# Half-bank pieces in a transformer block: the first exponential of a step in two operations, products and additions by 256 columns

## The chip, the cores and the metric

The kernel runs on one core of one Trainium2 chip. The core has five engines with queues of their own: TensorE (PE, matrix products into PSUM; its weight loads are listed apart as PEld), VectorE (DVE), ScalarE (ACT, exponentials and copies), GpSimd (POOL) and SyncE (SP, which issues the transfers). PSUM has eight banks of 512 fp32 columns over 128 partitions; SBUF is the working memory. The metric is the device time of one execution in microseconds (us). TensorE's weights for one product (`lhsT`) are loaded by an instruction of their own, and it can be addressed as four groups of 32 rows or four groups of 32 columns that work side by side.

## The reference

The input `x` has 8 batches of 1024 tokens and 256 features. All is fp32.

```python
mod = (silu(c) @ wmod).reshape(8, 6, 1, -1)
sa, ca, ga, sb, cb, gb = ...          # shifts, scales, gates; |gates| at least 0.25
h = layernorm(x) * (1 + ca) + sa
x = x + ga * attention(h)             # 16 heads of 16, causal softmax, output projection, bias
h = layernorm(x) * (1 + cb) + sb
x = x + gb * ffn(h)
# ffn, with the token before: h_prev
xr = mu_r * h + (1 - mu_r) * h_prev
xk = mu_k * h + (1 - mu_k) * h_prev
out = sigmoid(xr @ W_r.T) * (square(relu(xk @ W_k.T)) @ W_v.T)
```

## The kernel before

**Units and steps.** A unit is one batch and four of its heads; there are 32. The 1024 tokens are two chunks of 512 (`CW`), each of four blocks of 128 tokens. The attention of a unit goes in nine steps (`STEPS`, `ORDER`): five for blocks on the causal diagonal (a to e; b and d pair a piece of 128 queries with one of 384, c has two of 256) and four for whole blocks of the second chunk's queries against the first chunk's keys (0 to 3).

**What one step does.** `step` (L1122) interleaves two streams of score products on TensorE. The maxima of a later step (`maxima`, tiles `k,q` in the profile, nine steps ahead) put queries by keys into banks, and VectorE finds each row's largest. The weights of the present step (`weights`, tiles `q,k` and `m,ones`) put keys by queries into four banks, subtract the row's maximum by a third product, and `exponentials` (L685) turns each bank of 512 columns into weights `w` in SBUF by one ScalarE operation. The four heads make two halves of two heads, so there are four exponentials in a step, and POOL masks those on the diagonal. Score products use 32 rows of the array (forms `32*128`), so two heads of one stream and two of the other run side by side; the loop at L1149 to L1152 takes the next product from the half that has `took` fewer columns so far.

**What stands between the score products.** After a step's scores come the products in its slot (`fill`) and the attention `attend` (L710) of steps that are done: weights times values, four heads in four groups of 32 columns (form `128*32`). The slots hold the projections of the next batch (`qk`, `v`), the output projection of the batch before (`project`), and its feed-forward part (`receptance`, `key`, `multiplied`, `valued`), placed by tables of step numbers (`POST`, `PREP` and others). `by_strips` (L434) cuts such a product in four strips of 32 columns of the array. A product of fp32 shows as twice as many matmuls in the profile as in the program; the scores, fp32r, as one each.

**Order.** The lines of the code set the order on TensorE throughout. While `strict[0]` is set, which is nearly all of the kernel, they set it on every engine (`InOrder`; all operations therefore show one line, L160). Transfers go through `later` and `transfers` at the start of a step.

**Banks.** All PSUM is one tile, `banks` (L98). `bank` gives the bank that by the kernel's own account is free earliest, and `banks_of_step` plans those of a step's scores, with the first exponential's bank free first. So the first product after a step's scores, be it a projection, a transpose or an attention, commonly takes over the bank that the step's first exponential reads. The semaphore waits are made by the framework from what each instruction reads and writes.

**The edges.** `late[0]` is set from the step where no maxima are left (L1128): the last nine steps. A tail with operations of its own ends the kernel.

Of the kernel before, what the change touches and what calls it, by code (L numbers as in the profile page):

```python
# [10 lines left out]
AF = mybir.ActivationFunctionType  # L11
ALU = mybir.AluOpType
# [3 lines left out]
P = 128  # L16
# [37 lines left out]
FIRST, LAST = ("a", "f", "g"), ("e", "h", "i")  # L54
LAG = 9
BANKS = 8
PIECES = {0: NT, 1: 2 * NT}


# [15 lines left out]
def adaln_block(  # L75
# [235 lines left out]
    def v_tile(b, i):  # L311
        return v_of[(b * NC + i // NT) % (2 * NC)][:, i % NT]
# [141 lines left out]
                )  # L454


    def prep(b, c):
        S = A[b, c]

        def stats(*ts):  # L460
            statistics(S["xa"], S, f"a{b}_{c}", ts)

        def norm(half):
            normalise(S["xa"], S, f"a{b}_{c}", half)
            if half == 0:
                return
            nxt = b * NC + c + 1
            if 1 < nxt < B * NC:
                later(lambda: load_xa(nxt // NC, nxt % NC))

        def turn():
            S["hT"] = sb.tile([P, DC, CW], F32, tag="hT", bufs=2, name=f"hT{b}_{c}")
            for d in range(DC):
                name = f"pta{b}_{c}_{d}"
                transposed(S["h"], S["hT"][:, d, :], b, d, SHIFT_A, SCALE_A, name)

        def qk(n, half):

            pq = bank(f"pq{b}_{c}_{n}_{half}")
            at = n * D + half * P  # L480
            for d in range(DC):
                by_strips(
                    pq, wqk_sb[:, d, at : at + P], S["hT"][:, d, :], d == 0, d == DC - 1
                )
            w, hi = (
                sb.tile([P, CW], F32, tag="qk", bufs=4, name=f"qk{b}_{c}_{n}_{half}{h}")
                for h in range(2)
            )
            if n == 0:
                act.mul(w, pq, SCALE)  # L490
            else:
                act.copy(w, pq)
            hi, lo = hi.bitcast(F32R), w.bitcast(F32R)
            pool.tensor_copy(hi, w)
            pool.tensor_sub(lo, w, hi.bitcast(F32))

            def away():
                to = (q_in, k_in)[n][b % 2][half]
                for h, of in enumerate((hi, lo)):
                    sync.dma_start(to[:, h, c * CW : (c + 1) * CW], of.bitcast(F32))  # L500

            later(away)

        def v(t0):
            pv = bank(f"pv{b}_{c}_{t0}")
            rows(pv, S["hT"], wv_sb, (t0, t0 + 1))
            to = v_of[(b * NC + c) % (2 * NC)]
            act.copy(
                to[:, t0 : t0 + 2, : H * (HD + 1)].rearrange(
                    "p t (h e) -> p t h e", e=HD + 1  # L510
                )[:, :, :, :HD],
                pv.rearrange("p (t h e) -> p t h e", t=2, e=HD),
            )

        return dict(
            stats0=lambda: stats(0, 1),
            stats1=lambda: stats(2, 3),
            stat0=lambda: stats(0),
            stat1=lambda: stats(1),
            stat2=lambda: stats(2),  # L520
            stat3=lambda: stats(3),
            norm0=lambda: norm(0),
            norm1=lambda: norm(1),
            turn=turn,
            q0=lambda: qk(0, 0),
            k0=lambda: qk(1, 0),
            q1=lambda: qk(0, 1),
            k1=lambda: qk(1, 1),
            v0=lambda: v(0),
            v2=lambda: v(2),  # L530
        )
# [127 lines left out]
    def weights(u, k, half, pws):  # L659

        diagonal = STEPS[k][0][2]
        V = U[u]
        qs, kk = qs_of[u % KEPT], k_of[u % KEPT]
        js = (2 * half, 2 * half + 1)
        pw = pws[half]
        parts, total = parts_of(k)
        rounds = []
        for c, kt, lo, cols in parts:
            for h in range(3):

                def products(c=c, kt=kt, lo=lo, cols=cols, h=h):
                    for n2, j in enumerate(js):
                        at = j * ST
                        if h < 2:
                            rs = slice(at, at + ST)
                            left = kk[rs, kt * P : (kt + 1) * P]
                            right = qs[h][rs, c * CW + lo : (c + 1) * CW]
                        else:
                            left = ones[at : at + 2, :]
                            right = V["m", c][at : at + 2, lo:]  # L680
                        pe.matmul(pw[n2][:, cols], left, right, start=h == 0, stop=h == 2)

                rounds.append((CW - lo, products))

        def exponentials():  # L685
            w = sb.tile([P, 2, CW], F32, tag="w", bufs=8, name=f"w{u}_{k}_{half}")
            for n2 in range(2):
                act.activation(w[:, n2, :total], pw[n2][:, :total], AF.Exp)
            if diagonal:

                blocks = len(parts)
                apart = parts[-1][3].start or CW
                on = w.rearrange("p h (m q) -> p h m q", q=apart)[:, :, :blocks, :P]
                pool.affine_select(
                    out=on,
                    in_=on,
                    pattern=[[0, 2], [0, blocks], [1, P]],
                    compare_op=ALU.is_ge,
                    fill=0.0,
                    base=0,  # L700
                    channel_multiplier=-1,
                )
            V["w", k, half] = w

        return rounds, exponentials, 0
# [4 lines left out]
    def attend(u, k, then):  # L710

        c, steps, _ = groups_of(u)[k]
        V = U[u]
        b, g = divmod(u, NG)
        po = bank(f"po{u}_{k}")

        parts = sorted(
            ((at, *part[1:]) for at in steps for part in parts_of(at)[0] if part[0] == c),
            key=lambda part: part[2],
        )  # L720
        ws = {(at, half): V["w", at, half] for at in steps for half in range(2)}
        for m, (at, kt, lo, cols) in enumerate(parts):
            for j in range(HG):
                pe.matmul(
                    po[j * ST : (j + 1) * ST, lo:],
                    v_tile(b, kt)[:, (g * HG + j) * (HD + 1) :][:, :ST],
                    ws[at, j // 2][:, j % 2, cols],
                    start=m == 0,
                    stop=m == len(parts) - 1,
                )  # L730
        then()
        if ("o", c) not in V:
            V["o", c] = sb.tile([P, CW], F32, tag="o", bufs=3, name=f"o{u}_{c}")
            act.copy(V["o", c], po)
        elif strict[0]:
            more = sb.tile([P, CW], F32, tag="more", bufs=2, name=f"more{u}_{k}")
            act.copy(more, po)
            pool.tensor_add(V["o", c], V["o", c], more)
        else:
            dve.tensor_add(V["o", c], V["o", c], po)  # L740
# [88 lines left out]
    def post(b, c):  # L829
# [11 lines left out]
        def flat(t0):  # L841
            return S["x"][:, t0 : t0 + 2, :].rearrange("p t e -> p (t e)")

        def project(t0):
            py = bank_apart(f"py{b}_{c}_{t0}")
            rows(py, S["oT"], G[b]["wo"], (t0, t0 + 1))
            dve.tensor_add(flat(t0), flat(t0), py)

        def stats(*ts):
            statistics(S["x"], S, f"b{b}_{c}", ts)  # L850
# [55 lines left out]

        def key(e):
            pk = bank_apart(f"pk{b}_{c}_{e}")
            for d in range(DC):
                by_strips(  # L910
                    pk, wk_sb[:, d, e * P : (e + 1) * P], S["step"][:, d, :], d == 0, d == DC - 1
                )
            if e == 0:
                S["ka"] = sb.tile([P, DC, CW], F32, tag="mix", bufs=2, name=f"ka{b}_{c}")
            ka = S["ka"][:, e, :]
            act.activation(ka, pk, AF.Relu)
            pool.tensor_mul(ka, ka, ka)
# [7 lines left out]
        def valued(t0):  # L925
            r, pv = S["r", t0], S["pv", t0]

            dve.scalar_tensor_tensor(r, r, 1.0, pv, ALU.add, ALU.mult)
            pool.tensor_add(flat(t0), flat(t0), r)
            if t0:  # L930
                later(lambda: sync.dma_start(tokens(out, b, c), S["x"]))
# [190 lines left out]
    def step(T, T1, S, now, fill):  # L1122
# [26 lines left out]
        while any(lists):  # L1149
            s = min((s for s in range(2) if lists[s]), key=lambda s: (took[s], lists[s][0][3], s))  # L1150
            cols, products, after, _ = lists[s].pop(0)
            took[s] += cols  # L1152
            products()
            if after:
                after()
# [290 lines left out]
```

## Time and profile before

| | |
|---|---|
| time, median of 3 runs | 1377.53 us (1376.43 to 1382.0) |
| the profiled execution | 1386.23 us, its span 1384.5 us |
| granted TensorE clock, mean | 0.961 |
| DVE busy | 1056.9 us (76%) |
| ACT busy | 861.5 us (62%) |
| exponential of 512 columns | 0.60 us |
| DMA engines' mean busy share in a slice | 0 to 0.5 |

A row of the profile names engine, operation, tiles (`out<-in`, buffer numbers left out), shape and count, then the busy time and the mean duration. In the timeline a row begins with start and length in us, rows of the same kind that follow each other are merged (`x4`), and the brackets tell how long the engine was idle before and what released it. In the list of waits a row is: who waited for whom, us in total, times, longest. Matmuls are pipelined and the profile models their ends; their starts are recorded. A few per cent of the matmul records can be missing.

### The profile page before, as it was taken

The page shows a single profiled execution, that of the slowest core. Times are in us where ns is not written, and L with a number is a line of the kernel's source. Part 1 is how long each engine was busy: PE and PEld are TensorE (multiplying, and loading weights), DVE is VectorE, ACT ScalarE, POOL GpSimd, SP SyncE. Part 2 cuts the span into 40 slices and gives each one's busy share as a digit, 9 for nine tenths or more (in the row PEclk, how much of TensorE's full clock was granted, in tenths as well). Part 3 has the DMA queues.
Part 4 walks back from the last instruction along what each step waited for, and adds up shares of the span by engine and source line. Part 5 has one row for each costly group of instructions (what it writes and reads, how often), then busy time and mean ns, then how long its engine had stood idle before and what let it go on. Part 6 is the DMA issues. An engine that isn't in the chain of part 4 may idle for free.

```text
span 1384.5 us, 41749 instructions
## 1 busy us (share of the span) xinstructions
PE 1284.9 (93%) x16570; PEld 692.5 (50%) x16570; DVE 1056.9 (76%) x2910; ACT 861.5 (62%) x1679; POOL 710.7 (51%) x1088
## 2 busy tenths in 40 slices
PE   7898999999999899998999899998999989999988
PEld 4354555544455445554455454554455544544546
DVE  5776777788777877778777888778878788778745
ACT  2475677757567566765666666675666656656562
POOL 1334646546355556455565555564644556555352
PEclk8998999999999999999999999999999999999999
DMA  5114434422344323332434213443223323220111
GB/s 164 68 55 140 163 117 134 147 91 71 106 156 132 96 89 111 132 113 94 129 125 145 92 64 125 149 139 98 85 93 132 133 95 114 95 93 31 51 36 35
DMA packets 86515, 146.70 MB, mean 106 GB/s; under 512 B 12200, under 2 KB 42792, under 8 KB 86320
## 3 DMA queue, kind: packets, MB, share of 16 engines
q1 hardware_dynamic: 86112, 143.84, 31.4%
q8 instruction: 130, 2.13, 0.6%
q14 instruction: 65, 0.53, 0.1%
q10 hardware_dynamic: 208, 0.20, 0.0%
HBM read 86.35 MB, written 56.08 MB: 103 GB/s over the span
## 4 chain that ended last, share of the span: by engine, by line
PE 66%; DVE 9%; POOL 8%; ACT 7%; issue 5%; DMA 0%; POOLq 0%; DVEq 0%; ACTq 0%; SPq 0%
PE banks L160 66%; DVE mix L160 4%; ACT w L160 3%; DVE max L160 2%; POOL qk L160 2%; ACT w_e L160 1%; DVE banks L160 1%; POOL o L160 1%; POOL xb L160 1%; ACT w_d L160 1%; POOL oT L160 1%; POOL w_c L160 1%; POOL w_b L160 1%; POOL mrow L160 1%; POOL w_a L160 0%
## 5 line engine op out<-in xcount | busy, mean ns | idle before, releaser
L160 DVE CUSTOM_DVE_ANT_0 banks<-banks,mask 128x256 f32<-128x256 f32 (+3 forms) x1024 | 467.0, 525 | 121.9 <-PE banks L160 119.4
L160 PE MATMUL banks<-k,q 32*128 32x512 f32 (+3 forms) x3072 | 427.3, 371 | 5.8 <-DVE k L160 3.7
L160 PE MATMUL banks<-q,k 32*128 32x512 f32 (+3 forms) x3072 | 398.1, 369 | 5.4 <-ACT hT L160 1.2
L160 DVE TENSOR_REDUCE max<-banks 128x2 f32<-128x1024 f32 x256 | 302.5, 1221 | 91.7 <-PE banks L160 91.5
L160 PEld LDWEIGHTS banks<-q,k 32*128 32x128 f32 x3072 | 236.5, 185 | 149.0 <-ACT w L160 43.5
L160 ACT ACTIVATE w<-banks 128x512 f32<-128x512 f32 x512 | 264.2, 603 | 61.7 <-PE banks L160 58.4
L160 PE MATMUL banks<-m,ones 2*128 2x512 f32 (+3 forms) x1536 | 262.0, 351 | 8.7 <-DMA m<-mrow 8.7
L160 PEld LDWEIGHTS banks<-k,q 32*128 32x128 f32 x3072 | 252.0, 185 | 29.9 <-DVE max L160 5.9
L160 PEld LDWEIGHTS banks<-m,ones 2*128 2x128 f32 x1536 | 144.7, 185 | 16.1 <-DMA m<-mrow 7.1
L160 DVE DVE_READ_ACCUMULATOR2_ANT max<- 128x1 f32 x1024 | 143.2, 140 | 0.0
L160 PE MATMUL banks<-hT,wqk_sb 128*32 128x512 f32 x960 | 117.6, 610 | 10.6 <-ACT w_b L160 5.0
L160 PE MATMUL banks<-w,v 128*32 128x512 f32 x1024 | 123.2, 599 | 0.4 <-ACT w_a L160 0.2
L160 POOL TENSOR_TENSOR o<-o,more 128x512 f32<-128x512 f32 x62 | 79.2, 1277 | 69.0 <-ACT more L160 69.0
L160 PE MATMUL banks<-wr_sb,mix 128*32 128x256 f32 (+1 forms) x936 | 82.6, 502 | 27.9 <-DVE mix L160 27.7
L160 ACT ACTIVATE w_a<-banks 128x512 f32<-128x512 f32 x128 | 66.1, 602 | 36.3 <-PE banks L160 34.1
L160 POOL TENSOR_TENSOR qk<-qk,qk 128x512 fp32r<-128x512 f32 x60 | 81.0, 1350 | 5.0
L160 ACT ACTIVATE w_c<-banks 128x512 f32<-128x512 f32 x120 | 62.0, 602 | 24.7 <-PE banks L160 24.7
L160 DVE SCALAR_TENSOR_TENSOR mix<-step,mus,h2T 128x512 f32<-128x512 f32 x30 | 75.0, 2532 | 0.0
L160 POOL TENSOR_TENSOR xb<-xb,r 128x512 f32<-128x512 f32 x30 | 39.3, 1311 | 66.4 <-DVE r L160 55.6
L160 ACT ACTIVATE w_e<-banks 128x512 f32<-128x512 f32 x128 | 66.1, 604 | 10.0 <-PE banks L160 9.5
L160 ACT ACTIVATE w_d<-banks 128x512 f32<-128x512 f32 x120 | 62.0, 603 | 16.6 <-PE banks L160 14.6
L160 ACT ACTIVATE r<-banks 128x512 f32<-128x512 f32 x32 | 19.2, 600 | 84.8 <-PE banks L160 81.6
(166 smaller groups left out, 1993.6 us busy)
## 6 DMA issues: line engine op xcount, KB each, us to landing
q<-qin SPq DMA_DIRECT2D x60, 512.0 KB
qin<-qk SPq DMA_DIRECT2D x60, 256.0 KB
kin<-qk SPq DMA_DIRECT2D x60, 256.0 KB
k<-kin SPq DMA_DIRECT2D x30, 512.0 KB
od<-o SPq DMA_DIRECT2D x60, 256.0 KB
xa<-in_x SPq DMA_DIRECT2D x16, 512.0 KB
xb<-in_x SPq DMA_DIRECT2D x16, 512.0 KB
oT<-od SPq DMA_DIRECT2D x60, 128.0 KB
```

Of the source, the lines that this page charges most:

```text
L160: made = f(*args, **kwargs)
```

## The change

Five edits, all of order or of operation size; nothing is computed otherwise.

- The first exponential of each step (first half, first head) is done by two operations, columns 0 to 255 and the rest, while maxima are left (`not late[0]`).
- `columns` does the products of queries, keys and of the feed-forward keys (`qk`, `key`) for 256 columns first and then for the other 256. Before, one matmul had 512 columns.
- `attend` does all products that reach into the first 256 queries, then those of the last 256.
- VectorE adds the output projection to the rows of `x` (`project`) and forms (r + 1) times the values (`valued`) by two operations of 256 columns, while `strict[0]` is set.
- In `step`, a score product counts as at least 256 columns (`SHORT`) when the two halves are interleaved.

```diff
+SHORT = 256
+    def columns(to, lhs, rhs):
+        for of in (slice(0, CW // 2), slice(CW // 2, CW)):
+            for d in range(DC):
+                by_strips(to[:, of], lhs[:, d, :], rhs[:, d, of], d == 0, d == DC - 1)
...
         def qk(n, half):
-            for d in range(DC):
-                by_strips(
-                    pq, wqk_sb[:, d, at : at + P], S["hT"][:, d, :], d == 0, d == DC - 1
-                )
+            columns(pq, wqk_sb[:, :, at : at + P], S["hT"])
...
         def exponentials():
             for n2 in range(2):
-                act.activation(w[:, n2, :total], pw[n2][:, :total], AF.Exp)
+                parted = half == 0 and n2 == 0 and not late[0]
+                for of in (
+                    (slice(0, CW // 2), slice(CW // 2, total)) if parted else (slice(0, total),)
+                ):
+                    act.activation(w[:, n2, of], pw[n2][:, of], AF.Exp)
...
     def attend(u, k, then):
-        for m, (at, kt, lo, cols) in enumerate(parts):
-            for j in range(HG):
-                pe.matmul(
-                    po[j * ST : (j + 1) * ST, lo:],
-                    v_tile(b, kt)[:, (g * HG + j) * (HD + 1) :][:, :ST],
-                    ws[at, j // 2][:, j % 2, cols],
-                    start=m == 0,
-                    stop=m == len(parts) - 1,
-                )
+        for first in range(0, CW, CW // 2):
+            here = [part for part in parts if part[2] < first + CW // 2]
+            for m, (at, kt, lo, cols) in enumerate(here):
+                of = slice(max(lo, first), first + CW // 2)
+                cols = slice(cols.start + of.start - lo, cols.start + of.stop - lo)
+                for j in range(HG):
+                    pe.matmul(
+                        po[j * ST : (j + 1) * ST, of],
+                        v_tile(b, kt)[:, (g * HG + j) * (HD + 1) :][:, :ST],
+                        ws[at, j // 2][:, j % 2, cols],
+                        start=m == 0,
+                        stop=m == len(here) - 1,
+                    )
...
         def project(t0):
-            dve.tensor_add(flat(t0), flat(t0), py)
+            for of in halves():
+                dve.tensor_add(flat(t0)[:, of], flat(t0)[:, of], py[:, of])
+
+        def halves():
+            return (slice(0, D), slice(D, CW)) if strict[0] else (slice(0, CW),)
...
         def key(e):
-            for d in range(DC):
-                by_strips(
-                    pk, wk_sb[:, d, e * P : (e + 1) * P], S["step"][:, d, :], d == 0, d == DC - 1
-                )
+            columns(pk, wk_sb[:, :, e * P : (e + 1) * P], S["step"])
...
         def valued(t0):
-            dve.scalar_tensor_tensor(r, r, 1.0, pv, ALU.add, ALU.mult)
+            for of in halves():
+                dve.scalar_tensor_tensor(r[:, of], r[:, of], 1.0, pv[:, of], ALU.add, ALU.mult)
...
     def step(T, T1, S, now, fill):
-            took[s] += cols
+            took[s] += max(cols, SHORT)
```

## The prediction

> **What bounds the kernel now.** I read the page's busy shares first, then the waits, then the timeline of two typical steps, then the groups by shape.
>
> ```profile
> span 1384.5 us, 41749 instructions
> PE 1284.9 (93%) x16570; PEld 692.5 (50%) x16570; DVE 1056.9 (76%) x2910; ACT 861.5 (62%) x1679; POOL 710.7 (51%) x1088
> PE 66%; DVE 9%; POOL 8%; ACT 7%; issue 5%; DMA 0%; POOLq 0%; DVEq 0%; ACTq 0%; SPq 0%
> ```
>
> TensorE (PE) looks full, and PE holds 66% of the chain. But the ends of matmuls are modelled, so 93% hides short waits. The waits show which:
>
> ```profile
> PEld banks L160 <- ACT w L160: 77.9, 152, 0.9
> ...
> PEld banks L160 <- ACT w_b L160: 36.0, 58, 0.8
> ...
> PEld banks L160 <- ACT w_c L160: 24.5, 29, 2.2
> ...
> PEld banks L160 <- ACT w_a L160: 17.6, 38, 0.8
> ...
> PEld banks L160 <- ACT w_e L160: 14.6, 36, 0.7
> ```
>
> TensorE's next weights wait for an exponential (tiles w, w_a to w_e) 313 times, each time under a microsecond. One such place in the timeline (start, length, engine):
>
> ```profile
> 501.58 2.07 ACT L160 ACTIVATE w_b<-banks 128x512 f32<-128x512 f32 x4 [0.39 <-PE banks L160]
> 501.62 0.34 PE L160 MATMUL banks<-m,ones 2*128 2x384 f32 x2
> 502.23 1.92 PE L160 MATMUL banks<-hT,wqk_sb 128*32 128x512 f32 x16 [0.25 <-ACT w_b L160]
> 504.09 0.39 PE L160 MATMUL banks<-q,k 32*128 32x256 f32 x2
> ```
>
> A step's scores end at 501.62 + 0.34. The first of its four exponentials runs from 501.58 to 502.18 (0.60 us, below). The next product, a projection, starts at 502.23: 0.05 us after that exponential, whose PSUM bank it takes over. Then TensorE runs without a break into the next step at 504.09.
>
> I laid the timeline's PE and ACT rows of the whole span side by side. TensorE has 285 stretches of score products. After 229 of them the next product starts 0.05 us (159 times) or 0.145 us (70 times, mostly products that wait for two engines) after the end of the step's first exponential. No other wait is as regular. So the first exponential's end is on the path some 229 times, and what it gains or loses there moves the whole kernel.
>
> **The change part by part.**
>
> *First exponential in two.* 281 steps get one operation more (the built program has 1758 ACTIVATEs for 1477). Whether the path gains or loses hangs on what the next product waits for. In the built program every such product still has one wait for ScalarE, ahead of its first matmul, and its later matmuls, those of columns 256 to 511 too, have none for ScalarE. Resolving the semaphore counts, 268 of the 274 products that wait for an exponential after a step's scores wait for the second piece; those of before wait for the one operation. The first piece also waits, as before, for the bank's last matmul. So nothing starts earlier, and the product waits for two pieces in a row. Their price, from pairs and singles of the two shapes in the timeline:
>
> ```profile
> 501.58 0.60 ACT L160 ACTIVATE w_b<-banks 128x512 f32<-128x512 f32 x1 [0.39 <-PE banks L160]
> 501.58 1.09 ACT L160 ACTIVATE w_b<-banks 128x512 f32<-128x512 f32 x2 [0.39 <-PE banks L160]
> 1271.74 0.49 ACT L160 ACTIVATE w_f<-banks 128x384 f32<-128x384 f32 x1 [0.18 <-PE banks L160]
> 1271.74 0.87 ACT L160 ACTIVATE w_f<-banks 128x384 f32<-128x384 f32 x2 [0.18 <-PE banks L160]
> ```
>
> Two of 512 columns take 1.09 us, two of 384 take 0.87: 0.215 us per 128 columns and pair. Two of 256 then take 0.87 - 0.215 = 0.66 us. One of 512 takes 0.60. The second piece ends 0.06 us later than the whole did. Bounds: the pieces overlap fully, +0; they don't overlap, 2 x (0.49 - 0.11) - 0.60 = +0.16 us. I take 0.06, as the rows of 384 are the nearest. Of the 229 places, 13 stand in the step before one in which the receptance waits 0.8 to 2.4 us for VectorE's mix (24 waits, 27.7 us in all); that wait swallows the delay. 216 x 0.061 = +13.2 us. The three later exponentials shift by as much as the products between, so nothing comes twice; POOL's masks wait for the second piece too, but feed products of a later step.
>
> The Trainium skill, "ScalarE: Activation LUTs", section "What ACT_TABLE_LOAD costs", gives an ACTIVATE of N elements 186 ns + 0.833 N and an overlap of about 93 ns back to back. That would make the split cost 2 x 399 - 93 - 612 = 93 ns and the sum 216 x 0.093 = 20 us, as an estimate; the rows above overlap more, and I keep 13.2.
>
> The Trainium skill, "PSUM — Partial Sum Buffer", section "PSUM bank collisions raise a hardware error", wants PSUM guarded by bank and quadrant, not by address. It speaks against a release of half a bank and for the wait found in the program; a release by address would make the sum of rival B. No run here shows a collision.
>
> *Products of 512 columns by 256.* 1726 matmuls more. Compare a projection of 512 columns, from 502.23 to 504.09 above (16 rows), with values, which run by 256 columns already (32 rows), up to the next scores:
>
> ```profile
> 486.63 1.93 PE L160 MATMUL banks<-wvb,ka 128*32 128x256 f32 x32 [0.18 <-ACT w L160]
> 488.49 0.18 PEld L160 LDWEIGHTS banks<-q,k 32*128 32x128 f32 x2 [0.41 <-issue]
> ```
>
> 1.86 us each; to the nanosecond the 512s take 1.854, the 256s 1.864. So +0.01 us for each of some 215 products (60 q and k, 27 keys, 128 of weights and v): +2.2 us. Bounds 0 and twice that. The products begin by taking over the same bank, so this too is on the path.
>
> *SHORT.* A score product of 128 columns counts as 256 when the two halves of a step are interleaved. In the built program this changes the order in three kinds of step, some 110 times, by one pair of 128-column products passing another. A pair takes 0.11 us (500.52 to 500.63 in the timeline); if it stood on the path in the 57 steps with three-quarter blocks, +-6.3 us. But the pairs go to the other half's rows of the array, and in the row of now the moved pair starts before the last score of the first half in either order. I take 0.
>
> *VectorE's additions by 256.* 58 operations more. The second half has no wait for TensorE of its own: both wait for the whole product. A half takes 0.415 us in the tail, a whole 0.687: up to 2 x 0.415 - 0.687 = +0.14 us each, 58 x 0.14 = 8 us if all were on the path, 0 if none. VectorE is idle before these very operations (24.2 and 15.6 us), its next maxima wait for TensorE, and TensorE's matmuls show no wait for xb or r; I take 0. If that cover were gone, the 8 us would show.
>
> No DMA is added or moved. Sum: 13.2 + 2.2 = +15.4 us on the profiled execution's 1386.23, so 1401.6. That execution lay 8.7 us above the median of 1377.53; against the median I forecast 1393 us (+1.1%).
>
> **The rivals.**
> A. As forecast: the whole bank's wait, 0.04 to 0.08 us per place: 216 x 0.04 to 229 x 0.08 plus 0 to 4 for the products, 1386 to 1400.
> B. The other side: the next product goes ahead after the first piece. It would start at first piece's end, 0.60 - 0.39 = 0.21 us earlier, but not before about 0.1 us after the last score has streamed. That leaves 0.21 us in some 127 places, 0.18 in 24 values, 0.13 in 24 projections wo, 0.09 in 27 transposes, 0.06 in 27 attentions of whole blocks: 38 us. With +2.2: 1341. It decides as soon as the first matmul of such a product waits for the first piece; the built program says no.
> C. The delay is swallowed: VectorE (76% busy) or ScalarE itself sets the end of many steps. Half the places: +8, 1385; all: 1378. Against it: the regular 0.05 us.
> D. VectorE's halves come onto the path as well, its maxima later and so the banks: up to +8 on A, 1401 or a little more.
> E. The pieces hardly overlap (0.12 to 0.16 us per place): +26 to +35, with +2.2: 1406 to 1415. Nothing in the ACT rows looks so.
>
> **How the numbers follow.** Measurement of this kernel tells about 0.5% (6.9 us) from no change. Chances: A 0.66, B 0.05, C 0.13, D 0.11, E 0.05. Predicted 1393, that of A. The range takes A, D and the upper half of C: 1384 to 1404; B, E and full swallowing stay outside. Faster 0.05 (B). Within 0.5% (1370.6 to 1384.4): most of C, 0.11. Slower: A, D, E and the rest of C, 0.84.
>
> **What would show it.** In the profile after: first exponentials of 256 columns, about 0.28 us apart, the second ending about 0.66 us after the first began; the next product 0.05 or 0.145 us after that second end; the distance from a step's first score to the next product up by about 0.06 us; products of 256 columns within 0.02 us of before; VectorE's waits as they were. A product that starts before the second piece's end would prove B. The prediction is wrong if the weight loads' idle time after exponentials falls, or if a step's scores take another time for their new order.

## The result and the profile after

The changed kernel takes 1394.3 us (median of 4 runs, 1391.53 to 1394.45) against 1376.98 us (4 runs) for the kernel before beside it: a ratio of 1.0113, 95% interval 1.0086 to 1.0140. By that ratio it is some 15.6 us more; the two medians lie 17.3 us apart. (The ratios in this document are estimates over the single runs, not quotients of the medians.) The profiled execution took 1391.53 us.

The page of the kernel after, its first lines and the shares of the chain by engine:

```profile
span 1389.8 us, 49067 instructions
PE 1278.3 (92%) x20022; PEld 801.4 (58%) x20022; DVE 1061.2 (76%) x2968; ACT 879.3 (63%) x1960; POOL 711.3 (51%) x1088
PE 66%; DVE 9%; POOL 8%; ACT 7%; issue 6%; DMA 0%; POOLq 0%; DVEq 0%; ACTq 0%; SPq 0%
```

ScalarE has its 281 operations more (1960 for 1679), VectorE its 58, TensorE 3452 matmul records. The shares of the chain hardly move: they can't show a delay of 0.06 us at 217 places. The timeline can. It is the same step as in the prediction, of the kernel after; the ACT row is given three times, cut after one, after two and after all of the row's operations (start, length, engine):

```profile
507.98 0.38 ACT L161 ACTIVATE w_b<-banks 128x256 f32<-128x256 f32 x1 [0.39 <-PE banks L161]
507.98 0.66 ACT L161 ACTIVATE w_b<-banks 128x256 f32<-128x256 f32 x2 [0.39 <-PE banks L161]
507.98 2.13 ACT L161 ACTIVATE w_b<-banks 128x256 f32<-128x256 f32 x5 [0.39 <-PE banks L161]
508.00 0.34 PE L161 MATMUL banks<-m,ones 2*128 2x384 f32 x2
508.68 1.45 PEld L161 LDWEIGHTS banks<-hT,wqk_sb 128*32 128x32 f32 x32 [0.66 <-ACT w_b L161]
508.69 1.93 PE L161 MATMUL banks<-hT,wqk_sb 128*32 128x256 f32 x32 [0.32 <-ACT w_b L161]
```

The first piece ends at 508.36. Half of the bank has been read by then, and the product begins with columns of just that half. It starts at 508.69 all the same, 0.05 us after the second piece (508.64). From the step's last score to the product it was 0.61 us (501.62 to 502.23) and is now 0.69; the matmul's idle time grew from 0.25 to 0.32.

I took the starts of all TensorE records of both traces and made the sums that the prediction made. After a step's scores the next product starts at the known 0.05 or 0.145 us after the end of the second piece 217 times, and never so after the first. The trace also shows why the first piece can't release it in this program: of the 281 first exponentials, 279 have a first piece that updates no semaphore. The second piece alone signals, for both. From the first piece's start to the second's end it is 659 ns (median), where the whole operation took 598. Of the distances from a step's first score to the next product, by kind of step: 1953 ns became 2014, 1710 became 1764, 1794 became 1854, 1872 became 1935, 1720 became 1778. The time between a step's first score and the product after it, summed over 285 steps, went from 564.9 to 578.6 us, +13.7. This sum scatters: in the five kernels with a whole first exponential and an unsplit second (the one before and four of the experiments) it lies between 561.2 and 564.9 us. Compared step by step between the two traces, the median step is 60 ns longer, and the 276 steps that differ by less than 0.2 us sum to +12.5 us.

Yet the two profiled spans differ by 5.3 us only, not by 17. Most of the rest is in one kind of product. The stretches of the receptance (tiles wr_sb,mix) took 88.5 us in all before and 78.4 after, in matmuls that the change doesn't touch. Their row of the groups by shape, before:

```profile
L160 PE MATMUL banks<-wr_sb,mix 128*32 128x256 f32 x928 | 79.5, 502 | 27.9 <-DVE mix L160 27.7 <-ACT w L160 0.2
```

and after:

```profile
L161 PE MATMUL banks<-wr_sb,mix 128*32 128x256 f32 x928 | 69.7, 451 | 27.4 <-DVE mix L161 25.2 <-ACT w_c L161 2.0 <-ACT w L161 0.2
```

The same 928 matmuls are 10 us shorter. The granted clock differs there, and it changes from execution to execution (last section). So the times of single executions mislead here, and the sums over the steps are read beside them.

### The profile page after: what moved, and what is told of

The parts are those of the page before. It is cut to its first block, busy times and chain, and to the rows that moved or that the text cites. A ratio compares the mean times of both kernels' runs of the same rounds, so it can differ in the third digit from the quotient of the medians.

```text
span 1389.8 us, 49067 instructions
## 1 busy us (share of the span) xinstructions
PE 1278.3 (92%) x20022; PEld 801.4 (58%) x20022; DVE 1061.2 (76%) x2968; ACT 879.3 (63%) x1960; POOL 711.3 (51%) x1088
## 4 chain that ended last, share of the span: by engine, by line
PE 66%; DVE 9%; POOL 8%; ACT 7%; issue 6%; DMA 0%; POOLq 0%; DVEq 0%; ACTq 0%; SPq 0%
PE banks L161 66%; DVE mix L161 4%; ACT w L161 2%; ACT w_e L161 2%; DVE max L161 2%; DVE banks L161 1%; POOL qk L161 1%; POOL ka L161 1%; ACT w_b L161 1%; POOL o L161 1%; POOL xb L161 1%; POOL oT L161 1%; POOL mrow L161 1%; POOL w_a L161 0%; POOL rsb L161 0%
## 5 line engine op out<-in xcount | busy, mean ns | idle before, releaser
L161 ACT ACTIVATE w<-banks 128x256 f32<-128x256 f32 (+1 forms) x636 | 272.1, 525 | 59.9 <-PE banks L161 56.4
L161 PE MATMUL banks<-m,ones 2*128 2x512 f32 (+3 forms) x1536 | 266.1, 353 | 8.5 <-DMA m<-mrow 8.5
L161 PE MATMUL banks<-hT,wqk_sb 128*32 128x256 f32 x1920 | 118.0, 388 | 13.4 <-ACT w_b L161 6.6
L161 PE MATMUL banks<-w,v 128*32 128x256 f32 x2048 | 123.6, 382 | 0.5 <-ACT w_a L161 0.3
L161 PE MATMUL banks<-wr_sb,mix 128*32 128x256 f32 (+1 forms) x936 | 71.8, 451 | 27.4 <-DVE mix L161 25.2
L161 PEld LDWEIGHTS banks<-hT,wqk_sb 128*32 128x32 f32 x1920 | 57.2, 111 | 62.9 <-ACT w_b L161 15.8
L161 ACT ACTIVATE w_a<-banks 128x512 f32<-128x512 f32 (+1 forms) x160 | 68.1, 522 | 35.7 <-PE banks L161 33.5
L161 PEld LDWEIGHTS banks<-w,v 128*32 128x32 f32 x2048 | 60.8, 109 | 51.2 <-ACT w L161 11.0
L161 ACT ACTIVATE w_c<-banks 128x512 f32<-128x512 f32 (+1 forms) x150 | 64.1, 521 | 22.2 <-PE banks L161 22.1
L161 ACT ACTIVATE w_d<-banks 128x512 f32<-128x512 f32 (+1 forms) x150 | 63.9, 522 | 17.3 <-PE banks L161 15.2
```

The costliest lines, as they stand in the source:

```text
L161: made = f(*args, **kwargs)
```

## The experiments

Three theories of the 16 to 17 us were set against each other. T1, that of the prediction: the next product waits for all operations that read its bank, and two pieces end 0.06 us after one whole. T2: it is the time that a further operation takes on ScalarE, wherever it stands. T3: it is the products and additions by 256 columns. Beside them stood rival B, that the product goes ahead after the first piece. The first four kernels shared 19 runs of the kernel before (median 1372.64 us) on one chip, the other four shared 29 (1372.28 us) on another.

**The split alone.** The kernel before, with the first exponential in two and nothing else.

```diff
             for n2 in range(2):
-                act.activation(w[:, n2, :total], pw[n2][:, :total], AF.Exp)
+                parted = half == 0 and n2 == 0 and not late[0]
+                for of in (
+                    (slice(0, CW // 2), slice(CW // 2, total)) if parted else (slice(0, total),)
+                ):
+                    act.activation(w[:, n2, of], pw[n2][:, of], AF.Exp)
```

> The kernel before with the first exponential in two and nothing else. Theory 1 (the next product waits for the whole bank, so the second piece's later end, 0.06 us, is paid in some 216 places): +13 us on the 1377 of before, 1390. Theory 2 (ScalarE's own time is what counts, wherever the extra operation stands): the same here. Theory 3 (the products and additions by 256 columns are what costs): 1377. Theory B (the product goes ahead after the first piece, and something else ate the gain): faster than before, towards 1340.

Measured: 1393.91 us, ratio 1.0139 (1.0074 to 1.0205, 4 runs). That is more than the +13 expected, but these runs had low mean clocks (0.963 to 0.970); at their own clocks they lie 13.7 us over the kernel before (table below). The steps' sum is 577.0 us, +12.0 on the kernel before; step by step, leaving out differences of 0.2 us and more, it is +12.3. 229 next products start 0.05 or 0.145 us after the second piece, none after the first. Against B this run says less than the changed kernel does: its queries, keys and attentions still begin with products of 512 columns, which write the whole bank in any case. One part of five carries what the change costs.

**All but the split.** The changed kernel with the first exponential whole.

```diff
             for n2 in range(2):
-                parted = half == 0 and n2 == 0 and not late[0]
-                for of in (
-                    (slice(0, CW // 2), slice(CW // 2, total)) if parted else (slice(0, total),)
-                ):
-                    act.activation(w[:, n2, of], pw[n2][:, of], AF.Exp)
+                act.activation(w[:, n2, :total], pw[n2][:, :total], AF.Exp)
```

> The changed kernel with the first exponential whole again. Theories 1 and 2: what is left of the 17 us is products, order and additions, 2 to 4 us: 1379 to 1381. Theory 3: 1394 as changed. Theory B: slower than changed.

Measured: 1378.85 us, ratio 1.0036 (0.9998 to 1.0073, 10 runs). The four other edits together cost at most 10 us and perhaps nothing. T3 doesn't account for the slowdown: this interval and that of the split alone do not overlap, if only just. The steps' sum is 562.4 us; from here to the changed kernel, which differs by the split alone, the steps that differ by less than 0.2 us sum to +13.3 us.

**The split on the second exponential.** As many operations on ScalarE as in the changed kernel, but the bank that the next product waits for is read by one.

```diff
-                parted = half == 0 and n2 == 0 and not late[0]
+                parted = half == 0 and n2 == 1 and not late[0]
```

> The changed kernel, with the second exponential of a step in two in place of the first: ScalarE has the same operations and the same busy time as in the changed kernel. Theory 1: the bank of the second one is taken over after a product of about 1.86 us, so nothing is late but the transposes' second bank (some 30 places, 2 us): 1379 to 1382. Theory 2: 1394, as changed.

Measured: 1384.61 us, ratio 1.0069 (1.0035 to 1.0103, 10 runs): 5.8 us above the kernel without a split, where T1 gave 2, and 9.3 below the split alone, on the same chip. The same step in its timeline:

```profile
504.32 0.60 ACT L161 ACTIVATE w_b<-banks 128x512 f32<-128x512 f32 x1 [0.38 <-PE banks L161]
504.32 2.13 ACT L161 ACTIVATE w_b<-banks 128x512 f32<-128x512 f32 x5 [0.38 <-PE banks L161]
504.98 1.93 PE L161 MATMUL banks<-hT,wqk_sb 128*32 128x256 f32 x32 [0.24 <-ACT w_b L161]
```

ScalarE is busy for 2.13 us in a row, as in the changed kernel, but the product starts 0.66 us after the first exponential began, 0.06 us after its end, with 0.24 us of idle time. Where the second piece stands decides most of the price, not that there is one more operation. It was dearer than expected, though. About 1.8 us is where it was looked for: 29 blocks of transposes that follow a step's scores take over the first bank and then the second, and went from 1.075 to 1.137 us each. These blocks lie outside the steps' sum, which itself is 3.8 us above that of the kernel without a split; of the 3.8, 2.0 us are in steps that differ by less than 0.2 us, the rest in nine steps that scatter. A few kinds of step became about 0.02 us longer; I did not find why.

**Four pieces.** The dose: the first exponential in operations of 128 columns.

```diff
-                    (slice(0, CW // 2), slice(CW // 2, total)) if parted else (slice(0, total),)
+                    [slice(p, min(p + P, total)) for p in range(0, total, P)] if parted else (slice(0, total),)
```

> The changed kernel with the first exponential in four pieces of 128 columns (three in the steps of 384). Theory 1, from the rows of 512 and 384 columns (0.107 us less for each 128 columns): pieces 0.174 us apart, the last 0.27 us long, the fourth ends 3 x 0.174 + 0.27 = 0.79 us after the first began, 0.135 us later than the second piece of the changed kernel: 216 x 0.135 = +29 us, 1423. Theory 3: 1394. Theory B: earlier release of a quarter, no slower than changed.

Measured: 1419.48 us, ratio 1.0342 (1.0290 to 1.0395, 4 runs). The same step, the ACT row cut after the first piece and after the fourth:

```profile
515.28 0.28 ACT L161 ACTIVATE w_b<-banks 128x128 f32<-128x128 f32 x1 [0.39 <-PE banks L161]
515.28 0.79 ACT L161 ACTIVATE w_b<-banks 128x128 f32<-128x128 f32 x4 [0.39 <-PE banks L161]
516.12 1.93 PE L161 MATMUL banks<-hT,wqk_sb 128*32 128x256 f32 x32 [0.44 <-ACT w_b L161]
```

A quarter of the bank is read by 515.56, and the product waits until 0.05 us after 516.07. The fourth piece ends 785 ns (median) after the first began, 126 ns later than the second of two; 233 next products start 0.05 or 0.145 us after that. 233 x 0.126 = 29 us; the steps' sum rose by 26.7 over the changed kernel, the median by 25.2. Price and dose agree, and rival B is out. The product begins with 256 columns, which two of the four pieces read; the second of them ends 445 ns (median) after the first began. With B the product would have gone then, earlier than in the kernel before, where the whole exponential takes 598 ns. As in the changed kernel, the earlier pieces update no semaphore; the last signals for all.

**An uneven cut.** The changed kernel with the cut at column 384 where the exponential has 512.

```diff
-                    (slice(0, CW // 2), slice(CW // 2, total)) if parted else (slice(0, total),)
+                    (slice(0, 3 * CW // 4), slice(3 * CW // 4, total)) if parted and total == CW else (slice(0, total),)
```

> The changed kernel with the first exponential cut at column 384 in place of 256, where it has 512 columns. It tells whether the price of the split hangs on where the cut lies or on the second operation alone. Theory of the whole bank's wait with the pieces' overlap: the pieces start as far apart as two of 384 do (0.87 - 0.49 = 0.38 us), and the second, of 128 columns, ends about 0.28 us after its start (0.49 less 2 x 0.108 us), so 0.66 us after the first began, as in the changed kernel: 1394 us, within 3 us, the next product 0.05 or 0.145 us after the second piece's end. If a long first piece let the next product or the later banks go earlier: less than 1388. If the second piece had to wait for the first to end (no overlap): 0.49 + 0.28 = 0.77 us, 1418 us.

Measured: 1390.42 us, ratio 1.0116 (1.0073 to 1.0160, 4 runs). Its step, the ACT row cut after the first piece and after the second:

```profile
504.95 0.49 ACT L161 ACTIVATE w_b<-banks 128x384 f32<-128x384 f32 x1 [0.38 <-PE banks L161]
504.95 0.66 ACT L161 ACTIVATE w_b<-banks 128x384 f32<-128x384 f32 x2 [0.38 <-PE banks L161]
505.66 1.93 PE L161 MATMUL banks<-hT,wqk_sb 128*32 128x256 f32 x32 [0.31 <-ACT w_b L161]
```

The second piece ends 0.66 us after the first began wherever the cut lies (median 659 ns), and 219 next products start 0.05 or 0.145 us after it. At these two cuts the price is that of the second operation, about 0.06 us, and not of a size of piece. The time was a little under the 1391 to 1397 us expected, on a chip where the kernel before was 4.7 us faster; the ratio is that of the changed kernel.

**The small parts, one by one.** The kernel before with `columns` and the new `attend` alone:

```diff
+    def columns(to, lhs, rhs):
+        for of in (slice(0, CW // 2), slice(CW // 2, CW)):
+            for d in range(DC):
+                by_strips(to[:, of], lhs[:, d, :], rhs[:, d, of], d == 0, d == DC - 1)
...
+            columns(pq, wqk_sb[:, :, at : at + P], S["hT"])
...
+        for first in range(0, CW, CW // 2):
+            here = [part for part in parts if part[2] < first + CW // 2]
...
+            columns(pk, wk_sb[:, :, e * P : (e + 1) * P], S["step"])
```

> The kernel before with the products alone changed: queries, keys, feed-forward keys and attention by 256 columns; the exponentials whole, the additions whole, SHORT left out. By the prediction's term, about 0.01 us for each of some 215 products, +2.2 us; by the sums of the changed kernel's trace, +2.8 in attention and +0.7 in the other two, +3.5 us. Against the runs of the kernel before beside it, a ratio of 1.0016 to 1.0026. If instead the whole of the 5 us by which the changed kernel without its split stood above the kernel before were the products', 1.0036. If an early start of the second half's columns were worth something, under 1.0000.

Measured: 1376.38 us, ratio 1.0016 (0.9985 to 1.0047, 12 runs). The blocks that the change touches became longer by 0.010 us each, to the nanosecond alike in this kernel and the changed one: whole-block attention 1855 to 1865 ns, the other attentions 2291 to 2301, queries and keys 1842 to 1852, two keys of the feed-forward 3571 to 3591 (medians). Some 215 x 0.010 = 2.2 us. The +2.8 us that this expectation takes from the changed kernel's attention hold a few long blocks of up to 4 us as well, which the kernel before has too.

The kernel before with VectorE's additions in halves alone:

```diff
-            dve.tensor_add(flat(t0), flat(t0), py)
+            for of in halves():
+                dve.tensor_add(flat(t0)[:, of], flat(t0)[:, of], py[:, of])
...
-            dve.scalar_tensor_tensor(r, r, 1.0, pv, ALU.add, ALU.mult)
+            for of in halves():
+                dve.scalar_tensor_tensor(r[:, of], r[:, of], 1.0, pv[:, of], ALU.add, ALU.mult)
```

> The kernel before with VectorE's additions of the projections and of the values in two operations of 256 columns alone. The prediction: 0, with a bound of +8 us if all 58 of 0.14 us stood on the path. A ratio of 1.000 by the theory that VectorE's idle time covers them, 1.0058 by rival D. TensorE's waits for VectorE's tiles as in the kernel before.

Measured: 1376.14 us, ratio 1.0013 (0.9985 to 1.0041, 12 runs). Rival D's 1.0058 lies outside. The additions do take longer: a pair of halves 753 ns (median), a whole one 687, so 0.066 us each and not the bound of 0.14. All 58 on the path would be 3.8 us, a ratio of 1.0028, which this interval alone does not exclude. The trace does: the steps that differ by less than 0.2 us from those of the kernel before sum to +0.5 us. The weight loads of later scores wait more for the additions. The list of waits (who for whom, us, times, longest), before:

```profile
PEld banks L160 <- DVE xb L160: 4.9, 24, 0.6
PEld banks L160 <- DVE r L160: 4.4, 24, 0.2
```

and with the halves alone:

```profile
PEld banks L160 <- DVE xb L160: 6.9, 25, 0.8
PEld banks L160 <- DVE r L160: 6.3, 25, 0.4
```

That is 3.9 us more idle time of the weight loads, while neither list has a wait of TensorE's matmuls for xb or r. One thing is left: the attentions after whole blocks start some 0.02 us later at 28 places, 0.5 us in all, cause not found.

The kernel before with SHORT alone:

```diff
+SHORT = 256
...
-            took[s] += cols
+            took[s] += max(cols, SHORT)
```

> The kernel before with SHORT alone: the order of a step's score products. The prediction: 0, bounds of 6.3 us on both sides. The changed kernel's trace without its split showed one class of step, of 14 places, shorter by 0.04 us from its first score to the next product, 0.6 us in all; a ratio of 0.9996 by that, 0.9954 if each of 57 steps with blocks of three quarters gained a pair of 0.11 us, 1.0046 if each lost one. Everything else as in the kernel before.

Measured: 1373.45 us, ratio 0.9993 (0.9962 to 1.0023, 12 runs). Two kinds of step show it: 14 that end in queries or keys take 1720 ns for 1758 (medians), and two that end in transposes 2257 for 2083 and 2268 for 2198. That is -0.5 and +0.2 us: nothing that the time could show. So no part of the change, alone, makes the kernel faster by anything that can be measured, and there was no better version to build of them.

**All by the clock.** The mean granted clock stands with every execution, and the 48 of the kernel before lie on a line against it (last section), with 1.07 us around it. Distance of each kernel's runs from that line, at their own clocks, mean and standard error:

| kernel | us over the kernel before |
|---|---|
| changed | 19.0 +- 1.2 |
| split alone | 13.7 +- 0.9 |
| all but the split | 1.6 +- 0.3 |
| second exponential split | 6.2 +- 0.6 |
| four pieces | 44.5 +- 0.5 |
| uneven cut | 16.6 +- 0.8 |
| products alone | 1.2 +- 0.7 |
| halves alone | -0.8 +- 0.4 |
| SHORT alone | 0.4 +- 0.4 |

The split and the rest make 13.7 + 1.6 = 15.3 us, the forecast sum was 15.4. The changed kernel's own 19.0 lies 3.7 above; with four runs, which lie 15.8 to 21.6 us over the line, I leave that open.

A kernel in which the product may go ahead after the first piece was not tried: to take that wait away, the first matmuls would write a bank that ScalarE still reads.

## Why the prediction was right, point by point

- *What bounds the kernel.* Right in the count by starts, though not in the reading of the list before it. The list's 313 waits are not "each under a microsecond": the row of w_c has one of 2.2 us. And 124 of the whole list's 320 waits for exponentials, 69.7 us, are of loads for later scores (q,k), where the matmuls themselves are hardly idle (see the sign below). The first exponential's end sets the start of the next product at 229 places before, 217 after, 233 with four pieces, and what happened to that end moved the kernel in the amount worked out.
- *First exponential in two, +13.2 us.* Right in mechanism and size: the wait is for the second piece, as read in the built program's semaphores; 659 ns for the 0.66 us worked out from the rows of 384 and 512 columns; 12.3 to 13.3 us by the steps compared one by one. The bounds of +0 and +0.16 us per place both lay far off. That the places before the receptance swallow the delay is not contradicted, but not shown either: from their first score to the receptance it took 3.70 us before and 3.61 after (medians of 13), and from 3.24 to 3.76 in the other eight kernels, too much scatter to see 0.06 us.
- *The sum, 1393 us.* The split and the rest, each apart, make 15.3 us by the clock line, as forecast. That the changed kernel's own median, 1394.3, lies so near has some luck in it: by the same line it stands 19.0 us over the kernel before, and no run accounts for the 3.7 between.
- *The Trainium skill, "ScalarE: Activation LUTs", "What ACT_TABLE_LOAD costs".* Its duration and its overlap of about 93 ns back to back would have made the split 93 ns dear and the sum 20 us, as an estimate. The runs show 61 ns and 12.3 to 13.3 us: the measurement decides, and the rows of this kernel were the better source.
- *The Trainium skill, "PSUM — Partial Sum Buffer", "PSUM bank collisions raise a hardware error".* It speaks for a guard by bank. The program does make the product wait for all pieces, halves and quarters, in 217 and 233 places; the semaphore of the last piece is the means. What a product without that wait would do, no run here shows.
- *Products, +2.2 us.* Right: +0.010 us each.
- *SHORT, 0.* Right in the sum, but not because nothing moves: a gain of 0.5 us and a loss of 0.2 nearly cancel. So the sign "if a step's scores take another time for their new order" came up, at a size that changes nothing.
- *VectorE's halves, 0.* Right; the weight loads' waits for xb and r grew, and with the halves alone no wait of the matmuls for them appeared. Rival D needed 8 us and had at most 0.5. Its price was too high as well: a half in the tail takes 415 ns, but a pair in a row 753 and not 830.
- *The profiled execution lay 8.7 us above the median.* Right to forecast against the median, though the reason, the clock, was not named.
- *What would show it.* One sign was badly chosen. I wrote that the prediction is wrong if the weight loads' idle time after exponentials falls. In the list of waits it did fall. The two largest rows after, for 77.9 and 36.0 before:

```profile
PEld banks L161 <- ACT w L161: 66.9, 148, 0.9
PEld banks L161 <- ACT w_b L161: 29.5, 56, 0.7
```

and in the kernel with the products alone:

```profile
PEld banks L161 <- ACT w L161: 65.7, 150, 0.9
PEld banks L161 <- ACT w_b L161: 27.2, 58, 0.6
```

The fall is that of the products by 256 columns. The first load of the next scores follows the last load of a product of 512 columns after 838 ns of idle time, and that of a product of 256 after 412; the scores' matmuls themselves were idle for 0 ns in both cases. So the waits of the loads of q,k for exponentials sum to 69.7 us before (124 waits) and to 47.9 with the products alone (122), and none of this difference was a stall. Between kernels with the same products the sign holds: without the split the two rows are 63.8 and 27.6, with it 66.9 and 29.5. The loads of all other products show it plainly: their waits for exponentials rose from 104.0 us in the kernel before to 114.2 with the split alone.

- *Rivals.* B fell by the second piece's wait and by four pieces, C by the undiminished +0.06 us at the kinds of step listed above, D by the halves alone, E by 659 ns.

## What to carry to other kernels

Before an operation is split so that a consumer may start on the first half, look at what the consumer waits for in the built program: where its one signal comes from the last piece, as here, the split adds the second operation's overhead to the path and gains nothing. The price of a piece can be had from the trace of before, from the ends of pairs and singles of neighbouring sizes. Count a wait as a stall only where the matmul itself is idle; idle time of the weight loads moves with the shape of the products around it.

## What the runs showed of the hardware

The granted clock of TensorE dropped to half in spells of some microseconds, and not at the same places in each execution. Of the kernel before, the receptance near 507 us: first the PE rows of the timeline, then the busy times by stretch (from:to, length, PE, PEld, DVE, ACT, POOL, granted clock, DMA share, GB/s):

```profile
507.27 0.64 PE L160 MATMUL banks<-wr_sb,mix 128*32 128x256 f32 x8 [0.91 <-DVE mix L160]
508.86 6.15 PE L160 MATMUL banks<-wr_sb,mix 128*32 128x256 f32 x56 [0.95 <-DVE mix L160]
```

```profile
507.20:509.20 2.00, 0.98 (x12) 0.39 (x16) 2.00 (x2) 1.75 (x4) 2.00 (x2) 0.70 0.94 234
509.20:511.20 2.00, 2.00 (x24) 0.99 (x20) 2.00 (x11) 0.00 (x0) 0.70 (x2) 0.50 0.90 238
511.20:513.20 2.00, 2.00 (x27) 0.86 (x20) 1.95 (x8) 0.60 (x1) 0.00 (x0) 0.50 0.95 348
515.00:517.00 2.00, 1.65 (x39) 1.35 (x40) 1.24 (x3) 1.45 (x3) 0.00 (x0) 1.00 0.06 23
```

The same place after:

```profile
513.67 0.64 PE L161 MATMUL banks<-wr_sb,mix 128*32 128x256 f32 x8 [0.84 <-DVE mix L161]
515.26 3.23 PE L161 MATMUL banks<-wr_sb,mix 128*32 128x256 f32 x56 [0.95 <-DVE mix L161]
```

```profile
515.60:517.60 2.00, 2.00 (x44) 1.20 (x40) 2.00 (x11) 0.60 (x1) 0.70 (x2) 1.00 0.81 209
```

Both times TensorE waited twice for VectorE's mix, 0.84 to 0.95 us each. The 56 matmuls behind the second wait took 6.15 us in one execution, at a clock of 0.50, and 3.23 in the other, at 1.00. Over the twelve receptances of 64 matmuls in each of the two traces the blocks take from 4.74 to 7.66 us. What decides it, the runs don't tell; it is not the change alone, for each of the two traces has short and long blocks.

It is also most of the measurement's scatter. The 48 executions of the kernel before ran from 1365 to 1388 us at mean clocks of 0.975 to 0.959, correlated at -0.98, 1.4 us for each 0.001 of the clock; the two chips lie on one line, and the profiled execution of before, 1386.23 at 0.961, lies 0.5 us from it.
